# Gated projection of a graph network: products of pairs taken as seven of their own blocks' products, two at a time in shared PSUM banks that are refilled with sums

## The chip, the cores and the metric

One core of one Trainium2 chip. The metric is the device time of one execution in microseconds (us); the kernel before has a median of 2511.55 us over three runs (2511.07, 2511.55, 2512.0). Engines are called as the profile calls them: PE is TensorE's matmuls, PEld its weight loads, DVE VectorE, ACT ScalarE, POOL GpSimd, SP the queue that issues the DMAs.

## The reference

A pre-LN network on a graph of 1024 nodes with 512 features. A graph convolution, four layers, a graph convolution; the last output and two residuals are added. The layer, with LN for a layer norm with its weights:

```python
for i in range(4):
    h = h + _attn(LN2(h), cond, Wq[i], Wk[i], Wv[i], Wo[i])      # 16 groups of 64 nodes, 256 conditions each
    u = LN3(h) @ geglu_w[i] + geglu_b[i]                         # 1024 x 512 @ 512 x 4096
    val, gate = split(u, 2, axis=-1)
    f = val * gelu(gate)                                         # 1024 x 2048
    h = h + f @ ffo_w[i] + ffo_b[i]
```

The change concerns the second product, u, called the gated projection here. All of it is float32. The residual `base`, which the output stage adds at the very end, is relu(LN(x)) + x + gcn_out_b, and is made beside the layers.

## The kernel before

**Loops.** A layer l (of L = 4) first runs attention over eight groups of nodes g = 0 to 7, then the feed-forward part in R = 4 rounds r = 0 to 3. A round covers 512 of the 2048 columns of `val` and of `gate`, makes `f` for them (`geglu`), and adds its share of `f @ ffo_w` to h (`ffn_out`, two halves s = 0 and 1).

**Seven products.** Large matrix products are made by blocks of two by two, with seven block products in place of eight. The left factors are the weights `wval`, `wgate` and three sums of them (`ges`), made on GpSimd by `geglu_weights` for the next round; the right factors are the transposed normalised nodes `ln3T` and their sums `ln3S`. The products carry numbers 0 to 6 (the position in `order7`). One product for one block c of 128 columns is two matmuls of 128x512 (two contraction halves, `multiply`, L302), and it is collected in PSUM banks of 128x512 and combined by additions: value and gate of both halves of the nodes, f0 and f1, come out of seven products.

**Round 0** takes blocks c = 0 to 3 one after another (class `Quad`, `first`, `second`, `rest`).

**Rounds 1 to 3** take them in two pairs p = 0, 1 (class `Pair`), blocks p and p + 2 together: 24 pairs in the program. Here products 5 and 6 of the pair are made by seven products of their own blocks once more (`INNER = (5, 6)`): `Pair.seven` makes seven matmuls of 128x256 (L1021) which hold the answer for both blocks, with two banks e and f, each halved, and combines them by 128x256 operations (L1025 to L1038). The left factors of these inner products are further sums of the weights, made in `inner_lefts` on GpSimd for each round (three tiles, two inner products); the right ones are further sums of `ln3T` and `ln3S`, made in `inner_right_of` on GpSimd in round 0 and kept in `wos`, a tile that is free then. Products 0, 4, 3, 2 and 1 are direct: 20 matmuls of 128x512 for the two blocks. `Quad.end` finishes each block: the gate's sum (L964, L968), gelu on ScalarE (L933), the value's sum with its bias (L971), the product with the gate (L973, L975).

**After a block** `sums` in `geglu` makes the sums of f that `ffn_out` needs (L1083 to L1087); its last instruction, `geglu.last`, releases GpSimd for the next round's weights.

**ffn_out** is 14 products of four matmuls of 128x256, two halves of seven; its results are added to h (`hall`), s = 1 to blocks 2, 3, 6 and 7.

**The residual base** is made in the pairs of rounds 1 to 3, a block after each pair until eight are done: fetch x, Relu on ScalarE (L1396), two additions on GpSimd (L1398, L1399), a store to DRAM (L1400).

**Order.** Engines execute their own queues in order, and the order within them is the one in which the program issues, except where `issue_after` and `waiting_for` move something, and `keep_in_program_order` forbids it. `waiting_for(x, engine)` lets what follows on an engine stand after x. PSUM has eight banks, `bank(name)` gives the next; `acc_tile` gives one of six buffers of 128x512, `t512` one of ten; `slots_of` takes from 36 slots of 128x1024. `add_bias` adds the output bias row `ffb` to a block of h on GpSimd, for blocks 6 and 7 after round 0.

Of the kernel before, what the change touches and what calls it, by code (L numbers as in the profile page):

```python
# [8 lines left out]
F32 = mybir.dt.float32  # L9
# [5 lines left out]
OP = mybir.AluOpType  # L15
# [8 lines left out]
def gnn_kernel(  # L24
# [49 lines left out]
    rows = ctx.enter_context(tc.tile_pool(name="rows", bufs=2))  # L74
# [38 lines left out]
    def load_row(vec, offset, name):  # L113
        t = rows.tile([P, D], F32, tag="row", name=name)
# [182 lines left out]
    def multiply(to, left, right, cols_of, start):  # L297

        for n, (l0, l1, r0, r1) in enumerate(cols_of):
            at = to if len(cols_of) == 1 else to[:, n * (r1 - r0):(n + 1) * (r1 - r0)]  # L300
            for k in range(2):
                nc.tensor.matmul(at, left[:, k, l0:l1], right[:, k, r0:r1],  # L302
                                 start=start and n == 0 and k == 0,
                                 stop=n == len(cols_of) - 1 and k == 1, skip_group_check=True)
# [604 lines left out]
    class Quad:  # L909
# [49 lines left out]
        def end(self):  # L959

            n, c, bias = self.n, self.c, gcols[:, self.cv:self.cv + 1]
            pc, pd = bank(f"gc_{n}"), self.d
            g1 = t512(f"g1_{n}")
            nc.vector.tensor_tensor(g1, pd, self.u3, OP.add)  # L964
            self.gate(g1, n)
            self.product(3, pc, True)
            g0 = t512(f"g0_{n}")
            nc.vector.tensor_tensor(g0, pc, self.u3, OP.add)  # L968
            self.gate(g0, n)
            self.product(2, pd, False)  # L970
            nc.vector.scalar_tensor_tensor(self.u2, pd, bias, self.u2, OP.add, OP.add)  # L971
            f0, f1 = (self.fT[i][c // 2][:, c % 2, :] for i in range(2))
            nc.vector.tensor_tensor(f1, self.u2, g1, OP.mult)  # L973
            self.product(1, self.a, False)
            nc.vector.scalar_tensor_tensor(f0, self.a, bias, g0, OP.add, OP.mult)  # L975

# [13 lines left out]
    INNER = (5, 6)  # L990

    def inner_lefts(l, r, left):
        rooms = [t512(f"gi_{l}_{r}_{i}") for i in range(3)]
        rooms = [x[:, i * M:(i + 1) * M] for x in rooms for i in range(2)]
        return {i: inner_left(nc.gpsimd, left[i], *rooms[3 * n:3 * n + 3])
                for n, i in enumerate(INNER)}

    def inner_right_of(n, right):
        rooms = [wos[:, 2 * n + k, i * M:(i + 1) * M] for k in range(2) for i in range(2)]
        return inner_right(nc.gpsimd, right[INNER[n]], *rooms)  # L1000

    class Pair:

        def __init__(self, l, r, p, left, right, inner, fT):
            self.n, self.p, self.inner = f"{l}_{r}_{p}", p, inner
            self.quads = [Quad(l, r, c, left, right, fT) for c in (p, p + 2)]

        def seven(self, i):  # L1010

            n, p = f"{self.n}_{i}", self.p
            left, right = (x[i] for x in self.inner)
            e, f = bank(f"ge_{n}"), bank(f"gf_{n}")
            a, b, c, d = e[:, :M], e[:, M:], f[:, :M], f[:, M:]
            t = acc_tile(f"gt_{n}")
            to = self.w = [acc_tile(f"gw{q}_{n}") for q in range(2)]
            s1, u2 = t[:, :M], t[:, M:]

            def product(k, to, start):  # L1020
                nc.tensor.matmul(to, left[k][:, p * P:(p + 1) * P], right[k], start=start,  # L1021
                                 stop=True, skip_group_check=True)

            product(0, a, True)
            nc.scalar.copy(s1, a)  # L1025
            product(5, b, False)
            nc.vector.tensor_tensor(u2, b, s1, OP.add)
            product(6, c, True)
            nc.vector.tensor_tensor(s1, c, u2, OP.add)
# [11 lines left out]
        def run(self, sums, beside):  # L1041
            q0, q1 = self.quads
            for q in self.quads:
                q.a = bank(f"ga_{q.n}")
            q0.product(0, q0.a, True)
            steps = self.seven(5)
            next(steps)
            q1.product(0, q1.a, True)
            next(steps)
            for q, w in zip(self.quads, self.w):  # L1050
                q.u2 = w
                nc.vector.tensor_tensor(w, q.a, w, OP.add)
            steps = self.seven(6)
            next(steps)
            for q in self.quads:
                q.d = bank(f"gd_{q.n}")
            q0.product(4, q0.d, True)
            next(steps)
            for q, w in zip(self.quads, self.w):
                q.u3 = w  # L1060
                nc.vector.tensor_tensor(w, w, q.u2, OP.add)
            q1.product(4, q1.d, True)
            for q in self.quads:
                q.end()
                sums(q.c)
            beside(self.p)
# [10 lines left out]
    def geglu(quads, fT, s, begun, beside=lambda c: None):  # L1077
        def sums(c):
            k = c % 2
            a11, a12, a21, a22 = (fT[i][j][:, k, :] for i in range(2) for j in range(2))  # L1080
            s1, s2, s4 = (x[:, k, :] for x in s)
            if c < 2:
                nc.vector.tensor_tensor(a21, a11, a21, OP.subtract)  # L1083
            else:
                nc.vector.tensor_tensor(s2, a22, a21, OP.subtract)
                nc.vector.tensor_tensor(s1, s2, a11, OP.add)
                sums.last = nc.vector.tensor_tensor(s4, a12, s2, OP.subtract)  # L1087

        for c, q in enumerate(quads):
            if begun:  # L1090
                q.last = q.rest()()
                beside(c)
                sums(c)
            else:
                q.run(sums, beside)
        geglu.last = sums.last
        return order7([*fT[0], *fT[1]], *s)
# [164 lines left out]
    for l in range(L):  # L1262
# [63 lines left out]

        oTs = []
        for g in range(NG - 1):
# [8 lines left out]
            def between(last_key):  # L1337
# [9 lines left out]
                for nb in ready:  # L1347
                    add_bias(nb)

            if g or l:  # L1350
# [35 lines left out]
        fetched, rights = {}, {}  # L1386

        def fetch_x(nb):
            fetched[nb] = t512(f"x_again_{nb}")
            nc.sync.dma_start(fetched[nb], x[nb * P:(nb + 1) * P, :])  # L1390

        def base_of(nb):


            xt, xn = fetched.pop(nb), t512(f"again_{nb}")
            nc.scalar.activation(xn, xt, AF.Relu, bias=x_shift[:, nb:nb + 1],  # L1396
                                 scale=x_root[:, nb:nb + 1])
            nc.gpsimd.tensor_tensor(xt, xt, bias_out, OP.add)  # L1398
            nc.gpsimd.tensor_tensor(xt, xt, xn, OP.add)  # L1399
            nc.sync.dma_start(base_dram[nb], xt)  # L1400

        for r in range(R):
# [7 lines left out]
            if r:  # L1410
                fT, fS, quads = pairs_of(l, r, left, right, (lefts, rights))
                nb = 2 * (l * (R - 1) + r - 1)
                if nb < NB:
                    if nb == 0:
                        bias_out = load_row(gcn_out_b, 0, "bias_out")
                        nc.gpsimd.tensor_tensor(x_shift, x_mean.rearrange(
                            "p a (b c) -> p (a b) c", c=2)[:, :, 0], x_root, OP.mult)
                        nc.gpsimd.tensor_scalar(x_shift, x_shift, -1.0, None, OP.mult)
                    fetch_x(nb)
                    fetch_x(nb + 1)  # L1420
                    beside = lambda p: base_of(nb + p)
            else:
                wff = []

                def beside(c):
                    if c == 2:
                        wff.extend(out_weights(nc.vector, l, 0, raw_out))
                    elif c < 2:
                        with waiting_for(quads[c].last, mybir.EngineType.Pool):
                            rights[INNER[c]] = inner_right_of(c, right)  # L1430

            fT = geglu(quads, fT, fS, not r, beside)
            if r + 1 < R:
                raw_out = load_out(l, r + 1)
                with waiting_for(geglu.last, mybir.EngineType.Pool):
                    left = geglu_weights(l, r + 1, *raw)
                    lefts = inner_lefts(l, r + 1, left)
                    if not r:
                        for nb in range(NB - 2, NB):
                            add_bias(nb)  # L1440
                for s in range(2):
                    ffn_out(l, r, s, fT, wff, kept)
            else:
# [69 lines left out]
```

## Time and profile before

| | |
|---|---|
| median of three runs | 2511.55 us (2511.07 to 2512.0) |
| the profiled execution | 2511.2 us, of which the span that the profile shows is 2509.4 |
| PE busy | 2487.4 us, 99% |
| PEld | 1820.7 us, 73% |
| DVE | 1484.3 us, 59% |
| POOL | 619.8 us, 25% |
| ACT | 533.1 us, 21% |
| matmuls of the pairs, L302, by group `gd<-ln3S,ges` | 256 passes of 128x512, 128.1 us |
| matmuls of the inner seven, L1021, by group `ge<-ln3S,ges` | 96 passes of 128x256, 28.6 us |

A row of instructions gives line, engine, operation, output from inputs, the shape and the count, then busy time and the mean in ns of one, then the idle time of the engine ahead of it and what ended that. A row of a timeline begins with the start and the duration in us; one row may hold several instructions of a kind (x4). A float32 matmul shows as two instructions, called passes below. Matmul passes overlap in the pipeline, so a pass's own duration is longer than the distance to the next one's start.

### The profile page before, as it was taken

Reading aid. Unit: us, or ns where it says so; the run is one execution under the profiler, and the core shown is the slowest. Engines: PE = TensorE matmul, PEld = TensorE weight load, DVE = VectorE, ACT = ScalarE, POOL = GpSimd, SP = SyncE. Lnnn points to the kernel's source line nnn. Section 1 sums busy time; section 2 is a strip of 40 time slices with the busy share of each in tenths; the row PEclk is TensorE's granted clock in tenths of the full one; section 3 lists DMA queues with packets and bytes.
Section 4 is the critical chain, followed back from the end, with each engine's and each line's share of the span. In section 5 each row is a group of like instructions: output and inputs, shape, how many; then the busy total and the mean of one; then the engine's idle time right before and its main releaser. Section 6 shows DMA issues by size and latency. Waiting matters only on the chain. (4 is left out here: it accounts for less than half of the span.)

```text
span 2509.4 us, 33048 instructions
## 1 busy us (share of the span) xinstructions
PE 2487.4 (99%) x12752; PEld 1820.7 (73%) x12752; DVE 1484.3 (59%) x3265; ACT 533.1 (21%) x1318; POOL 619.8 (25%) x581
## 2 busy tenths in 40 slices
PE   8999999999999999999999999999999999999998
PEld 5778886666678887566687888566677888566665
DVE  9655565566664555666574555655574555665561
ACT  7322222111112222111112222211112222211111
POOL 1322223443220113332420113133401112233300
PEclk9999999999999999999999999999999999999999
DMA  6302232111211112020202222110121111111210
GB/s 180 132 30 93 93 110 68 47 68 34 105 59 61 59 64 68 23 86 17 97 30 76 72 64 59 43 43 26 51 76 59 60 62 65 43 42 51 84 34 34
DMA packets 69380, 161.06 MB, mean 64 GB/s; under 512 B 5768, under 2 KB 6096, under 8 KB 69216
## 3 DMA queue, kind: packets, MB, share of 16 engines
q1 hardware_dynamic: 67120, 153.44, 18.7%
q0 software_dynamic: 1376, 4.30, 0.5%
q8 instruction: 105, 1.72, 0.3%
q10 hardware_dynamic: 720, 1.11, 0.1%
q14 instruction: 59, 0.48, 0.1%
HBM read 135.76 MB, written 23.07 MB: 63 GB/s over the span
## 5 line engine op out<-in xcount | busy, mean ns | idle before, releaser
L302 PE MATMUL ga<-ln3T,wval 128*128 128x512 f32 x512 | 245.6, 593 | 0.0
L302 PEld LDWEIGHTS ga<-ln3T,wval 128*128 128x128 f32 x512 | 96.0, 190 | 89.5 <-issue 85.1
L933 ACT ACTIVATE g<-g,gcols 128x512 f32<-128x512 f32 x128 | 87.3, 716 | 328.8 <-DVE g L946 112.6
L777 ACT ACTIVATE pr<-sc,nmax 128x256 f32<-128x256 f32 x256 | 118.0, 473 | 176.7 <-DVE nmax L772 176.7
L302 PE MATMUL gd<-ln3S,ges 128*128 128x512 f32 x256 | 128.1, 592 | 0.0
L302 PE MATMUL pa_v<-wv,ct 128*128 128x256 f32 x512 | 123.1, 379 | 0.0
L220 POOL TENSOR_TENSOR ges<-wgate,wgate 128x1024 f32<-128x1024 f32 x16 | 37.7, 2353 | 344.3 <-DVE fs L1087 329.1
L302 PE MATMUL fa<-wff,fT 128*128 128x256 f32 x512 | 121.6, 379 | 0.0
L302 PE MATMUL pc_v<-wv,ct 128*128 128x256 f32 x512 | 121.0, 379 | 0.0
L302 PE MATMUL pc_k<-ct,wk 128*128 128x256 f32 x512 | 121.0, 379 | 0.0
L302 PE MATMUL pd_k<-ct,wks 128*128 128x256 f32 x512 | 121.0, 379 | 0.0
L302 PE MATMUL pd_v<-wvs,ct 128*128 128x256 f32 x512 | 120.9, 379 | 0.0
L302 PE MATMUL gd<-ln3T,ges 128*128 128x512 f32 x256 | 120.7, 594 | 0.1
L302 PE MATMUL gc<-ln3S,wgate 128*128 128x512 f32 x256 | 120.3, 592 | 0.0
L302 PE MATMUL pa_k<-ct,wk 128*128 128x256 f32 x480 | 116.2, 385 | 0.0
L302 PEld LDWEIGHTS fa<-wff,fT 128*128 128x128 f32 x512 | 97.3, 190 | 21.8 <-issue 9.1
L302 PEld LDWEIGHTS pc_k<-ct,wk 128*128 128x128 f32 x512 | 97.3, 190 | 13.2
L302 PEld LDWEIGHTS pd_v<-wvs,ct 128*128 128x128 f32 x512 | 97.3, 190 | 13.2
L302 PEld LDWEIGHTS pd_k<-ct,wks 128*128 128x128 f32 x512 | 97.3, 190 | 13.2
L302 PEld LDWEIGHTS pa_v<-wv,ct 128*128 128x128 f32 x512 | 97.1, 190 | 13.5 <-issue 0.4
L302 PEld LDWEIGHTS pc_v<-wv,ct 128*128 128x128 f32 x512 | 95.7, 190 | 12.2
L302 PEld LDWEIGHTS pa_k<-ct,wk 128*128 128x128 f32 x480 | 88.7, 190 | 21.3 <-issue 10.4
(354 smaller groups left out, 4962.3 us busy)
## 6 DMA issues: line engine op xcount, KB each, us to landing
ct<-cond_dram SPq DMA_DIRECT2D x72, 512.0 KB, 4.4
wval<-in_L_gnn_geglu_w_dram SPq DMA_DIRECT2D x32, 512.0 KB, 4.4
wgate<-in_L_gnn_geglu_w_dram SPq DMA_DIRECT2D x32, 512.0 KB, 4.7
wff<-in_L_gnn_ffo_w_dram SPq DMA_DIRECT2D x32, 512.0 KB, 4.0
cond_dram<-ct SPq DMA_DIRECT2D x24, 512.0 KB, 3.0
cond<-in_L_gnn_cond_dram SPq DMA_DIRECT2D x32, 256.0 KB, 4.5
ct<-cond_dram SPq DMA_DIRECT2D x24, 256.0 KB, 5.2
wk<-in_L_gnn_Wk_dram SPq DMA_DIRECT2D x8, 512.0 KB, 5.3
```

The lines of the kernel that those rows point to most:

```text
L220: t.tensor_tensor(s1, a21, a22, OP.add)
L302: nc.tensor.matmul(at, left[:, k, l0:l1], right[:, k, r0:r1], start=start and n == 0 and k == 0, stop=n == len(cols_of) - 1 and k == 1, sk ...
L777: nc.scalar.activation(pr3[:, a, :], ps3[:, a, :], AF.Exp, bias=nmax[:, a:a + 1], accum_out=tot[:, a:a + 1])
L933: nc.scalar.activation(pre, pre, AF.Gelu, bias=gcols[:, cg:cg + 1])
```

## The change

In rounds 1 to 3, products 0 and 4 of a pair are taken by inner sevens too: `INNER = (0, 5), (6, 4)`. `seven_of(two)` replaces `seven(i)`. It makes the seven inner products of two of the pair's products side by side, in four banks a to d, each holding 256 columns of the one and 256 of the other, and combines them by operations of 128x512. The results stand in `wos`, w for the first call and the same place for the second.

Products 1, 3 and 2 remain direct (12 matmuls of 128x512 for two blocks). They don't get banks of their own: after a `seven_of`, ScalarE copies sums back into its banks (L1057, L1059, L1065), and the direct products accumulate on top (`start=False`). So a bank ends with the finished value, and f is one operation per block and half (L1050) that reads it.

The matmuls of a pair are kept in program order. The sums of the first pair's f are issued within the second pair (after its second seven's last addition, L1067), those of the second at the round's end.

The tile `wos` being taken, the inner right factors live in four further slots (all 36 are then in use). Inner lefts take six tiles instead of three. The residual base moves from the pairs to attention, groups 1 and 2 of each layer; its additions are on VectorE, its buffers come from `acc_tile`. The shift `x_shift` is made on VectorE. The pool of bias rows has one buffer instead of two, with `bias_out` in one of its own. The output bias for blocks 6 and 7 is added in round 3, after its `geglu`, instead of round 0.

```diff
-    rows = ctx.enter_context(tc.tile_pool(name="rows", bufs=2))
+    rows = ctx.enter_context(tc.tile_pool(name="rows", bufs=1))
...
-    INNER = (5, 6)
+    INNER = (0, 5), (6, 4)
 
     def inner_lefts(l, r, left):
-        rooms = [t512(f"gi_{l}_{r}_{i}") for i in range(3)]
+        rooms = [t512(f"gi_{l}_{r}_{i}") for i in range(6)]
...
+        def seven_of(self, two):
+
+            p, (lefts, rights) = self.p, self.inner
+            a, b, c, d = (bank(f"g{x}_{self.n}_{two[0]}") for x in "abcd")
+            w = [wos[:, 2 * q:2 * q + 2, :] for q in range(2)]
+            s1, u2 = (acc_tile(f"g{x}_{self.n}_{two[0]}") for x in ("s", "u"))
 
             def product(k, to, start):
-                nc.tensor.matmul(to, left[k][:, p * P:(p + 1) * P], right[k], start=start,
-                                 stop=True, skip_group_check=True)
+                for n, i in enumerate(two):
+                    tc.keep_in_program_order(
+                        nc.tensor.matmul(to[:, n * M:(n + 1) * M],
+                                         lefts[i][k][:, p * P:(p + 1) * P], rights[i][k],
+                                         start=start and n == 0, stop=True, skip_group_check=True))
+
+            def add(to, x, y):
+                return nc.vector.tensor_tensor(to, of(x), of(y), OP.add)
...
             product(0, a, True)
             nc.scalar.copy(s1, a)
-            product(5, b, False)
-            nc.vector.tensor_tensor(u2, b, s1, OP.add)
+            product(5, b, True)
+            add(of(u2), b, s1)
             product(6, c, True)
-            nc.vector.tensor_tensor(s1, c, u2, OP.add)
-            product(4, d, False)
-            nc.vector.tensor_tensor(to[1][:, M:], d, s1, OP.add)
-            yield
+            add(of(s1), c, u2)
+            product(4, d, True)
+            add(w[1][:, :, M:], d, s1)
             product(1, a, False)
-            nc.scalar.copy(to[0][:, :M], a)
+            nc.scalar.copy(w[0][:, :, :M], of(a))
             product(3, c, False)
-            nc.vector.tensor_tensor(to[1][:, :M], c, u2, OP.add)
+            add(w[1][:, :, :M], c, u2)
             product(2, d, False)
-            nc.vector.tensor_tensor(to[0][:, M:], d, u2, OP.add)
-            yield
...
+            self.last = add(w[0][:, :, M:], d, u2)
+            return (a, b, c, d), [[x[:, n, :] for x in w] for n in range(2)]
...
+            def gated(q, of, w, name):
+                g = t512(f"{name}_{self.n}_{q}")
+                nc.vector.tensor_tensor(g, of, w, OP.add)
+                value, gate = biases(q)
+                nc.scalar.activation(g, g, AF.Gelu, bias=gate)
+
+                def times(to, x):
+                    nc.vector.scalar_tensor_tensor(to, x, value, g, OP.add, OP.mult)
+
+                return times
+
+            (a0, a1, c1, c0), (w1, w6) = self.seven_of(INNER[0])
+            a, c = (a0, a1), (c0, c1)
+            for q in (1, 0):
+                nc.scalar.copy(a[q], w1[q])
+                nc.vector.tensor_tensor(w6[q], a[q], w6[q], OP.add)
+                nc.scalar.copy(c[q], w6[q])
+            (*d, _, _), (w7, w5) = self.seven_of(INNER[1])
+            upper = {}
+            for q in (1, 0):
+                product(1, 1 - q, a[1 - q])
+                nc.vector.tensor_tensor(w5[q], c[q], w5[q], OP.add)
+                nc.scalar.copy(d[q], w5[q])
+                upper[q] = gated(q, d[q], w7[q], "g1")
+            with tc.issue_after(self.last.ins):
+                sums()
+            f = [[self.fT[i][n // 2][:, n % 2, :] for n in self.cols] for i in range(2)]
+            for q in range(2):
+                product(3, q, c[q])
+                gated(q, c[q], w7[q], "g0")(f[0][q], a[q])
+            for q in range(2):
+                product(2, q, d[q])
+                upper[q](f[1][q], d[q])
...
+        def base_of(nb):
+
+
+            xt, xn = fetched.pop(nb), acc_tile(f"again_{nb}")
+            nc.scalar.activation(xn, xt, AF.Relu, bias=x_shift[:, nb:nb + 1],
+                                 scale=x_root[:, nb:nb + 1])
+            nc.vector.tensor_tensor(xt, xt, bias_out, OP.add)
+            nc.vector.tensor_tensor(xt, xt, xn, OP.add)
+            nc.sync.dma_start(base_dram[nb], xt)
...
+                if g in (1, 2):
+                    base_of(2 * l + g - 1)
+
+            if g in (1, 2):
+                fetch_x(2 * l + g - 1)
...
+                with waiting_for(geglu.last, mybir.EngineType.Pool):
+                    for nb in range(NB - 2, NB):
+                        add_bias(nb)
                 ffn_out(l, r, 0, fT, wff, kept)
```

More of the change, by code (lines that the diff above doesn't have):

```diff
@@ L957, in rest @@
             return lambda: nc.vector.scalar_tensor_tensor(f0, self.a, bias, g0, OP.add, OP.mult)
[L959 to L975, printed above, removed]
     def inner_left(t, x, s1, s2, s4):
@@ L1007, in __init__ @@
             self.n, self.p, self.inner = f"{l}_{r}_{p}", p, inner
[L1008 to L1018, printed above, removed]
-            def product(k, to, start):
-                nc.tensor.matmul(to, left[k][:, p * P:(p + 1) * P], right[k], start=start,
-                                 stop=True, skip_group_check=True)
+            self.cols = [p, p + 2]
@@ L1094, in geglu @@
             else:
-                q.run(sums, beside)
+                q.run(sums_of_made)
+                made.extend(q.cols)
+        sums_of_made()
         geglu.last = sums.last
@@ L1385, in gnn_kernel @@
         kept = slot(f"kept_{l}")
[L1386 to L1400, printed above, removed]
+        rights = {}
         for r in range(R):
```

93 lines of the change are left out of this document (41 added, 52 removed).

## The prediction

> **What bounds the kernel now.** I read the page first, then TensorE's waits, then windows in three stages, and last the timeline of one pair of round 1.
>
> ```profile
> span 2509.4 us, 33048 instructions
> PE 2487.4 (99%) x12752; PEld 1820.7 (73%) x12752; DVE 1484.3 (59%) x3265; ACT 533.1 (21%) x1318; POOL 619.8 (25%) x581
> PEclk9999999999999999999999999999999999999999
> ```
>
> TensorE is busy for 2487.4 of 2509.4 us; no other engine passes 60%. Is the rest spread over the span or at its ends?
>
> ```profile
> PE edges L394 <- DVE high L380: 3.8, 1, 3.8
> ...
> PE deg L498 <- DVE sums L497: 0.5, 1, 0.5
> ```
>
> The view of TensorE's waits has ten rows, all of lines 302 to 656, each met once or twice: the graph stages at start and end. None is of the layers' projections.
>
> ```profile
> 488.00:560.00 72.00, 72.00 (x255) 47.98 (x254) 44.02 (x72) 9.72 (x18) 29.31 (x24) 1.00 0.19 66
> 800.00:900.00 100.00, 100.00 (x724) 86.52 (x723) 53.51 (x128) 24.51 (x73) 12.71 (x17) 1.00 0.19 64
> 1100.00:1200.00 100.00, 100.00 (x354) 66.80 (x353) 62.48 (x102) 12.22 (x22) 32.84 (x24) 1.00 0.11 37
> ```
>
> Columns: length, then busy time of PE, PEld, DVE, ACT, POOL, the clock granted, DMA. In a gated round (first row), in attention (second) and in a later stretch (third) TensorE is busy for the whole window at clock 1.00. So between the ends a matmul saved is its whole time saved, and each moment that TensorE waits is its whole time lost. Removing work from VectorE, ScalarE or GpSimd is worth nothing by itself.
>
> **What a matmul costs.** The timeline of one pair gives spacings; the durations in it overlap, so I use starts.
>
> ```profile
> 501.90 1.88 PE L302 MATMUL gc<-ln3S,wgate 128*128 128x512 f32 x4
> ...
> 506.20 1.02 PE L302 MATMUL ga<-ln3T,wval 128*128 128x512 f32 x2
> ...
> 513.92 0.59 PE L1021 MATMUL ge<-ln3S,ges 128*128 128x256 f32 x2
> ...
> 535.41 1.89 PE L302 MATMUL fa<-wff,fT 128*128 128x256 f32 x8
> ...
> 559.59 1.45 PE L302 MATMUL ga<-ln3T,wval 128*128 128x512 f32 x3
> ```
>
> A float32 matmul shows as two passes. Between 501.90 and 513.92 lie 28 passes of 512 columns (a pair's last seven products over two halves): 12.02/28 = 0.4293 us. Between 535.41 and 559.59, an output stage, lie 14 products of 8 passes of 256: 24.18/112 = 0.2159, and 1.727 for a product. So a matmul takes 0.8586 us at 512 columns and 0.4318 at 256, slightly more than half.
>
> **The change on TensorE.** There are 4 layers x 3 rounds x 2 = 24 pairs. In each, products 0 and 4 of two column blocks over two halves, 8 matmuls of 512 columns, become 2 x 7 = 14 of 256 (in the built program 192 fewer and 336 more). Removed 8 x 0.8586 = 6.869 us, added 14 x 0.4318 = 6.045: 0.824 less, of 20 x 0.8586 + 14 x 0.4318 = 23.22. Times 24: **19.8 us** less. With a short pass 1 ns shorter or longer it would be 0.7 us more or less.
>
> **Does TensorE stay without gaps?** Now banks are reused within a pair, so hand-offs to ScalarE and VectorE stand close to TensorE. Their rows:
>
> ```profile
> 493.07 0.42 DVE L1027 TENSOR_TENSOR gt<-ge,gt 128x256 f32<-128x256 f32 x1 [3.18 <-PE ge L1021]
> 493.53 0.42 DVE L1029 TENSOR_TENSOR gt<-gf,gt 128x256 f32<-128x256 f32 x1
> ...
> 503.36 0.69 DVE L964 TENSOR_TENSOR g<-gd,gw 128x512 f32<-128x512 f32 x1
> 503.97 0.68 DVE L968 TENSOR_TENSOR g<-gc,gw 128x512 f32<-128x512 f32 x1
> ...
> 506.40 0.75 DVE L971 SCALAR_TENSOR_TENSOR gw<-gd,gcols,gw 128x512 f32<-128x512 f32 x1 [1.15 <-PE gd L302]
> 507.24 1.45 DVE L973 TENSOR_TENSOR fT<-gw,g 128x512 f32<-128x512 f32 x1
> ...
> 511.73 0.69 DVE L973 TENSOR_TENSOR fT<-gw,g 128x512 f32<-128x512 f32 x1
> ```
> ```profile
> 504.14 1.95 ACT L933 ACTIVATE g<-g,gcols 128x512 f32<-128x512 f32 x3 [4.25 <-DVE g L964]
> ```
> ```profile
> 493.55 0.37 PEld L1021 LDWEIGHTS ge<-ln3S,ges 128*128 128x128 f32 x2 [0.49 <-DVE gt L1027]
> ```
> ```profile
> L1025 ACT COPY gt<-ge 128x256 f32<-128x256 f32 x48 | 17.9, 372 | 321.8 <-PE ge L1021 321.8
> L731 ACT COPY v<-pa_v 128x512 f32<-128x512 f32 x31 | 18.1, 585 | 193.6 <-PE pa_v L302 193.6
> L933 ACT ACTIVATE g<-g,gcols 128x512 f32<-128x512 f32 x128 | 87.3, 716 | 328.8 <-DVE g L946 112.6 <-DVE g L964 102.2 <-DVE g L968 97.2
> L1083 DVE TENSOR_TENSOR fT<-fT,fT 128x512 f32<-128x512 f32 x32 | 25.3, 789 | 0.8
> L220 POOL TENSOR_TENSOR ges<-wgate,wgate 128x1024 f32<-128x1024 f32 x16 | 37.7, 2353 | 344.3 <-DVE fs L1087 329.1 <-DVE pr L782 9.4 <-DMA cond_dram<-ct 5.9
> L222 POOL TENSOR_TENSOR gi<-gi,wgate 128x256 f32<-128x256 f32 x12 | 8.7, 727 | 0.0
> L213 POOL TENSOR_TENSOR wffs<-wff 128x512 f32<-128x512 f32 x12 | 15.2, 1271 | 0.0
> ```
>
> Hops: TensorE's slot end to VectorE 506.20 to 506.40, 0.20 us, and I take ScalarE alike. VectorE's end to ScalarE 504.05 to 504.14, 0.09, taken for the way back too. VectorE to a VectorE operation that needs it 493.49 to 493.53, 0.04; independent ones start 0.60 apart. VectorE's end to the weight load 493.49 to 493.55 and the load, 0.25. An addition of 128x512 takes 0.69, a copy out of PSUM 0.585. **The refill, a ScalarE copy into PSUM, is in no row.** Its nearest rows are the copy of half the size from below (0.372) and the gelu from above (0.716); far off, a GpSimd operation of that size, 1.271. I take 0.585, the same engine, size and operation with the ends exchanged, and keep 0.372 and 1.27 as ends; by the lower one nothing changes, since slack grows.
>
> Now a pair with 0 at its first matmul. The first seven for two products ends at 6.05, the second at 12.09; direct products 1 end at 15.52, 3 at 18.96, 2 at 22.39. Three places are tight.
>
> *Second seven, bank c.* The first seven's last addition (L1012) runs 6.25 to 6.94; ScalarE refills a (L1057) 7.03 to 7.61, and only behind that copies the next seven's first bank (L1018), 7.61 to 8.20; additions that need one another run 8.29 to 8.98 and 9.02 to 9.71; with 0.25 TensorE may accumulate into c at 9.96, and comes there, five slots of 0.864 after 6.05, at 10.36. Slack 0.40.
>
> *Direct product 3 into c.* That seven's addition out of c (L1012) runs 11.43 to 12.12, the addition L1064 on it 12.16 to 12.85, the seven's last 12.76 to 13.45, the refill of d (L1065) meanwhile 12.94 to 13.52, the gate's sum (L1045) 13.61 to 14.30, the other L1064, which reads the bank that product 3 wants, 14.21 to 14.90, with 0.25 at 15.15. TensorE comes at 15.52: slack 0.37. In a second pair the built order puts the first pair's subtraction L1092 ahead of that gate's sum: started at 13.36, it holds VectorE for 0.71 (its mean is 0.10 over the others'), so the sum starts at 14.07, the other L1064 ends at 15.36, and 15.61 is **0.08 late**: 12 x 0.08 = 1.0 us.
>
> *Round's end.* Two operations on f and four sums stand behind the last matmul. The second output product (24.11) needs L1092, done at 22.99 + 0.25: slack 0.87. The third, at 25.84, needs L1095, done at 25.11 + 0.25: slack 0.48.
>
> **The rest of the change.** Per round GpSimd makes 16 instead of 8 inner sums of 128x256 of the weights (in round 0 also 16 for 8 of the inputs, 16 x 0.727 = 11.6 us, read only after the output stage). It starts them when the round's last sum is done, about 3.4 us after the output stage begins, where it was
>
> ```profile
> 538.36 2.35 POOL L220 TENSOR_TENSOR ges<-wgate,wgate 128x1024 f32<-128x1024 f32 x1 [5.33 <-DVE fs L1087]
> ```
>
> 538.36 - 535.41 = 2.95 before. Up to the first sum that TensorE needs it has 4 x 2.35 + 7 x 0.727 + 1.27 = 15.8, so 19.2; the output stage lasts 24.18 and product 5 comes 0.86 later. Slack 5.8. The last sums, 27, meet a need at 24.18 + 6.05 + 0.86 = 31.1. If GpSimd's operations took a quarter longer, the first would still be in time. The additions of the bias to blocks 6 and 7, moved to round 3 and waiting on GpSimd for the round's last sum, are 2 x 1.27 from 3.4, done near 6; the output stage's second half, which adds to those blocks, starts at 12. Behind them in GpSimd's queue stand sums for the next layer's weights, which are wanted after the whole output stage. The next layer's bias row waits for its one buffer, and is wanted a layer later. Nothing of it costs.
>
> The residual base (16 additions of 128x512) leaves GpSimd for VectorE in attention:
>
> ```profile
> L302 PE MATMUL pc_v<-wv,ct 128*128 128x256 f32 x512 | 121.0, 379 | 0.0
> ```
>
> Those 512 passes are 16 for each of 32 projections: a product lasts 16 x 0.2159 = 3.45 us. Two additions are 2 x 0.79 = 1.6 us in front of one that frees a bank for a following product, on an engine with 53.51 of 100 us busy. Taken as hidden; uncovered it is 16 x 0.79 = 12.6 us. On SP's queue the base's store waits for these additions ahead of the loads of the block after next; seven products, 24 us, of the next block lie between, and the additions would have to be that late to matter.
>
> The addition L973, both of whose inputs lie in SBUF, took 0.69 us at 511.73 but 1.45 at 507.24, beside this:
>
> ```profile
> 506.87 1.26 POOL L1398 TENSOR_TENSOR x_again<-x_again,bias_out 128x512 f32<-128x512 f32 x1 [15.00 <-ACT again L1396]
> ```
>
> The moved additions have two such inputs too: at 1.45 the uncovered price is 23.2 us, and two of them, 2.9 us, still fit a product's 3.45. The Trainium skill, "SBUF — State Buffer", section "Who interferes with whom", has this as a rule: a VectorE instruction with two SBUF inputs contends with a GpSimd instruction that reads SBUF, one with a single such input does not. By that rule, the trace agrees.
>
> **The sum.** 2511.2 (the profiled execution: its span of 2509.4 and 1.8 around it) - 19.8 + 1.0 = 2492.4; that execution stood 0.35 under the median 2511.55, so **2492.8**.
>
> **Rivals.** *B, VectorE becomes the bound at the bank hand-offs.* For it: slacks of 0.4 are two hops wide, the bank's turn-round is a chain of five operations that no row of before shows end to end, L973's 1.45 is what a subtraction such as L1092 costs beside GpSimd, and VectorE has 26 operations of some 0.7 us in a second pair, 18 of 22.4 us (44.02 of 72 in the window of before). Against it: GpSimd's sums end at 27, long before a second pair begins at 24.18 + 22.39 = 46.6. If L1092 takes 1.45, the second pairs are late by 0.08 + 0.76: 12 x 0.84 = 10.1, 2501.9. If each chain is 0.5 us longer, first pairs lose 0.10 + 0.13, second 0.10 + 0.58: 12 x 0.91 = 10.9, **2502.7**.
>
> *C, slower: the refill copies.* A write into PSUM that takes x longer than 0.585 counts twice in the chain to the second seven, since two refills of a stand ahead of the copy there (the first ends at 6.75, the next starts at 7.03: 2x - 0.28 - 0.40), and once before product 3 (x - 0.37). The pair loses its 0.824 at 3x = 1.87: a refill of 0.585 + 0.625 = **1.21 us** is the point from which it is slower. At 1.27, x = 0.685: 0.69 + 0.31 = 1.00 per pair, 24.1 us, **2515.8**; at twice the gelu's 0.716, 2527. Against it: no ScalarE row of this size exceeds 0.72.
>
> The Trainium skill, "ScalarE: Activation LUTs", section "Step-by-step: what each stage is for", holds that PSUM is the lower-latency destination for ScalarE. No row here shows it; by it the refill is under 0.585, C falls away, and the sum stays, since in second pairs L1092 holds VectorE.
>
> *D, no gain in the passes.* It then doesn't do what it says. Short passes leave 0.2159 - 0.189 = 27 ns for the weight load, and in the pairs some loads stand idle for a releaser (11.7 us in the row of L1021's loads). If each of the 56 short passes took 0.824/56 = 15 ns more, the gain would be gone: **2511.5**. Against it: the pairs of before have such loads and no TensorE idle time, and 112 short passes in a row kept 0.2159.
>
> **How the numbers follow.** Forecast 0.69, B 0.20, C 0.07, D 0.04. The measurement tells 0.2%, 5 us, from no change: under 2506.5 is faster, which holds the forecast and nearly all of B (0.89); no change is D with a mild C (0.04); slower is C (0.07). The forecast's own range is 2490 to 2495: down without the lateness (1.0), by 0.7 for the spacings and 0.5 for the spread of the runs before, which makes 2490.6, rounded down; up by twice the lateness and the same two. Upwards the range reaches to B, 2503. C and D, 0.11, are left out.
>
> **What would show it.** Right would be: TensorE's waits without a row of the pairs, or one at L302 met about 12 times for 0.1 us; a pair's first matmul 22.4 us after the last one's; refills (L1057, L1059, L1065) near 0.585; L1092 at 0.69 in second pairs. Refills over 0.9, or TensorE waits on L1012, L1064 or L1018 in all pairs, would show it wrong; so would windows in attention, or at the start of a round's pairs, with TensorE below 100%.

## The result and the profile after

| | before | after |
|---|---|---|
| median of the runs | 2511.31 us (2509.79 to 2512.0, four runs) | 2491.39 us (2490.8 to 2492.21, four runs) |
| the profiled execution | 2511.2 us, span 2509.4 | 2491.68 us, span 2489.9 |

The changed kernel takes 0.9922 of the time (95% interval 0.9905 to 0.9939): 19.9 us less. The forecast was 2492.8 in 2490.0 to 2503.0, and 2492.4 for a profiled execution.

The page of the kernel after, its first two lines:

```profile
span 2489.9 us, 33837 instructions
...
PE 2468.3 (99%) x13040; PEld 1877.5 (75%) x13040; DVE 1517.5 (61%) x3235; ACT 635.5 (26%) x1462; POOL 686.4 (28%) x691
```

Of the span's 19.5 us, TensorE's busy time gave 19.1, with 288 more passes. ScalarE and GpSimd do 102 and 67 us more and VectorE 33, and TensorE waits for none of it in the layers. The waits of TensorE (line, who ended it, total, times, longest), first and last row of eleven:

```profile
PE edges L395 <- DVE high L381: 3.8, 1, 3.8
...
PE tr_x L184 <- DVE x L172: 0.2, 1, 0.2
```

There is still no row of the layers' projections. The same three windows as before (length; PE, PEld, DVE, ACT, POOL; clock; DMA):

```profile
488.00:560.00 72.00, 72.00 (x288) 54.37 (x287) 45.22 (x68) 17.49 (x29) 29.83 (x31) 1.00 0.15 46
800.00:900.00 100.00, 100.00 (x723) 86.47 (x722) 55.47 (x138) 25.81 (x75) 14.74 (x18) 1.00 0.22 77
1100.00:1200.00 100.00, 100.00 (x395) 74.73 (x394) 63.78 (x97) 20.90 (x34) 43.40 (x41) 1.00 0.12 34
```

TensorE is at 100% in all three, so the time must have gone out of the number and length of its passes. One round in the timeline of TensorE, kernel after, from the first pair's start through the second pair and the output stage to the next pair:

```profile
489.24 0.59 PE L1007 MATMUL ga<-ln3T,wval 128*128 128x256 f32 x2
...
501.32 1.88 PE L302 MATMUL ga<-ln3T,wval 128*128 128x512 f32 x4
...
511.62 0.59 PE L1007 MATMUL ga<-ln3T,wval 128*128 128x256 f32 x2
...
527.14 1.88 PE L302 MATMUL gd<-ln3S,wgate 128*128 128x512 f32 x4
...
534.01 1.89 PE L302 MATMUL fa<-wff,fT 128*128 128x256 f32 x8
...
558.18 0.59 PE L1007 MATMUL ga<-ln3T,wval 128*128 128x256 f32 x2
```

The first pair takes 511.62 - 489.24 = 22.38 us (22.39 before rounding), the second 22.39; its two sevens end 12.09 us after its start, and direct product 3 starts at 527.14, 15.52 into the pair. The forecast had 22.39, 12.09 and 15.52, with 15.61 for product 3 in second pairs. The same round before began here:

```profile
489.00 1.88 PE L302 MATMUL ga<-ln3T,wval 128*128 128x512 f32 x4
```

and ended at 559.59, the output stage's end that the prediction quotes: 70.59 us, against 68.94 now. That is 1.65 us in two pairs, and 12 rounds make 19.8. The whole gain is there. Between the last matmuls of one output stage and the next, all twelve such rounds of the profile after take 68.95 us, and eleven of the twelve before 70.59 (one takes 71.00). All first pairs of the profile after last 22.39 us, and second pair and output stage together 46.56 in each of the eight rounds that another round of pairs follows.

How the hand-offs stand to TensorE, VectorE's timeline in that second pair (511.62 is its start):

```profile
524.38 0.68 DVE L1012 TENSOR_TENSOR wos<-gd,gu 128x512 f32<-128x512 f32 x1
524.98 0.68 DVE L1092 TENSOR_TENSOR fT<-fT,fT 128x512 f32<-128x512 f32 x1
525.57 0.68 DVE L1045 TENSOR_TENSOR g<-gb,wos 128x512 f32<-128x512 f32 x1
526.17 0.68 DVE L1064 TENSOR_TENSOR wos<-gd,wos 128x512 f32<-128x512 f32 x1
```

L1092 starts at 13.36, as forecast. But it holds the queue for 0.59 us, not 0.71, so L1064 ends at 15.23 instead of 15.36. In a first pair, where L1092 doesn't stand, the rows of VectorE and ScalarE show the hops around the refill of d:

```profile
501.38 0.69 DVE L1064 TENSOR_TENSOR wos<-gc,wos 128x512 f32<-128x512 f32 x1
...
502.11 0.59 ACT L1065 COPY gb<-wos 128x512 f32<-128x512 f32 x1 [1.68 <-DVE wos L1064]
...
502.73 0.69 DVE L1045 TENSOR_TENSOR g<-gb,wos 128x512 f32<-128x512 f32 x1
```

From VectorE's end to ScalarE's start it is 0.04 us, and back 0.03; the forecast had 0.09 for each. The groups of instructions (busy us and the mean ns of one stand between the bars) give the price that no row of before showed:

```profile
L1026 ACT COPY wos<-ga 128x512 f32<-128x512 f32 x48 | 28.1, 585 | 105.1 <-PE ga L1007 105.1
...
L1059 ACT COPY gc<-wos 128x512 f32<-128x512 f32 x24 | 14.2, 593 | 0.0
L1065 ACT COPY gb<-wos 128x512 f32<-128x512 f32 x24 | 14.2, 591 | 40.2 <-DVE wos L1064 40.2
L1057 ACT COPY gb<-wos 128x512 f32<-128x512 f32 x24 | 14.2, 590 | 23.2 <-DVE wos L1012 23.2
```

A refill takes 590 to 593 ns, a copy out of PSUM 585. The forecast had taken 585.

### The profile page after: what moved, and what is told of

Read it like the earlier page. It is cut to its first block, busy times and chain, and to the rows that moved or that the text cites. A ratio compares the mean times of both kernels' runs of the same rounds, so it can differ in the third digit from the quotient of the medians.

```text
span 2489.9 us, 33837 instructions
## 1 busy us (share of the span) xinstructions
PE 2468.3 (99%) x13040; PEld 1877.5 (75%) x13040; DVE 1517.5 (61%) x3235; ACT 635.5 (26%) x1462; POOL 686.4 (28%) x691
## 5 line engine op out<-in xcount | busy, mean ns | idle before, releaser
L1342 POOL TENSOR_TENSOR hall<-hall,ffb 128x512 f32<-128x512 f32 x32 | 41.0, 1287 | 322.3 <-DVE xn_ln L172 238.3
L302 PE MATMUL ga<-ln3T,wval 128*128 128x512 f32 x224 | 104.4, 594 | 0.0
L1018 ACT COPY gs<-ga 128x512 f32<-128x512 f32 x48 | 27.9, 582 | 287.6 <-PE ga L1007 287.6
L849 POOL TENSOR_TENSOR os<-oT 128x256 f32<-128x256 f32 x12 | 8.7, 728 | 317.3 <-DVE oT L824 317.3
L1047 ACT ACTIVATE g<-g,gcols 128x512 f32<-128x512 f32 x96 | 69.3, 722 | 94.8 <-DVE g L1045 94.8
L773 DVE TENSOR_REDUCE nmax<-sc 128x2 f32<-128x512 f32 x128 | 83.0, 680 | 10.2 <-PE sc L766 10.2
```

Source lines behind the costliest of these rows:

```text
L302: each(nc.tensor.matmul(at, left[:, k, l0:l1], right[:, k, r0:r1], start=start and n == 0 and k == 0, stop=n == len(cols_of) - 1 and k == ...
L773: nc.vector.tensor_reduce(nmax, ps3, AX.X, OP.max, negate=True)
L849: t.tensor_tensor(s1, a21, a22, OP.add)
L1047: nc.scalar.activation(g, g, AF.Gelu, bias=gate)
L1342: nc.gpsimd.tensor_tensor(h[nb], h[nb], ffb, OP.add)
```

## The experiments

All run beside the kernel before on the same chip, whose median was 2510.93, 2511.93 or 2511.28 us in the three sets. "Over the changed kernel" means over its 2491.39 from the set of the result. The kernel before moved by up to 1.0 us between sets, so a difference of one or two us rests on the lengths of pairs and rounds in the trace, not on the medians.

### The parts around the pairs, alone

```diff
 kernel before
-                    beside = lambda p: base_of(nb + p)
...
+                if g in (1, 2):
+                    base_of(2 * l + g - 1)
```

> The kernel before with one part of the change alone: the residual base made in attention on VectorE, one row buffer, the output bias of blocks 6 and 7 added in round 3. The pairs are as before. If the forecast's step is right that all of this is hidden, the time is that of before, 2511.3 us within 1, and TensorE's waits have no row of the attention. If the two additions are uncovered, 16 x 0.79 = 12.6 us more. If the change gained by this part and not by its matmuls, the time falls towards 2491.

Measured: 2510.97 us, ratio 1.0001 (0.9992 to 1.0010). The residual base in attention, the single row buffer and the late bias cost nothing and bring nothing that could be measured (the interval reaches some 2.3 us to each side). So the gain is that of the pairs, and the price of 12.6 us for uncovered additions falls.

### What a short pass costs

```diff
-                         [(self.cols[q] * P, (self.cols[q] + 1) * P, 0, 512)], False,
+                         [(self.cols[q] * P, (self.cols[q] + 1) * P, m * M, (m + 1) * M)
+                          for m in range(2)], False,
```

> The changed kernel with each direct matmul of 128x512 in the pairs as two of 128x256: 12 become 24 per pair, the columns are the same. By the spacings (0.8586 and 0.4318) a pair takes 12 x 0.005 = 0.06 us more, 24 pairs 1.4 us: 2492.8. If short passes in a pair cost 15 ns more each than the forecast takes (rival D), 48 passes x 24 pairs x 0.015 = 17 us more. If a short pass costs exactly half, no change.

Measured: 2493.05 us (2492.09 to 2493.39), 1.7 over the changed kernel, against 1.4 expected and 17 by rival D. In its profile the direct part of a pair takes 10.36 us instead of 10.30: 0.06, the third digit of the spacings. Here columns are paid for and hardly instructions: 288 more matmuls cost 1.7 us. That is why taking products as sevens of half-width matmuls gains nearly the full eighth (0.824 of 6.869 us).

### The subtraction ahead of the hand-off

```diff
-            with tc.issue_after(self.last.ins):
+            with tc.issue_after(read.ins):
                 sums()
```

where `read` is the second L1064.

> The changed kernel, with the first pair's subtraction L1092 moved behind the second L1064 of the second pair. The forecast put it 0.08 us in the way in each of 12 second pairs, 1.0 us; the profile after shows no TensorE wait there and L1092 at 0.59 in the queue, so now: 2491.4, no change within 0.7 us, and the first L1064 to product 3 gets 0.6 us of slack. If hand-offs of VectorE bind as rival B has it, the time falls by several us.

Measured: 2491.47 us (2490.98 to 2492.04). No change: the hand-off wasn't late.

```diff
             if c < 2:
-                nc.vector.tensor_tensor(a21, a11, a21, OP.subtract)
+                if not begun:
+                    tc.keep_in_program_order(
+                        nc.vector.tensor_tensor(s1, a11, a21, OP.subtract))
+                tc.keep_in_program_order(nc.vector.tensor_tensor(a21, a11, a21, OP.subtract))
```

The gate's sums and the last addition of a seven are kept in program order too, and `sums()` is issued right behind the second seven. The added line runs for both pairs of a round, so the sums at the round's end come later as well.

> The changed kernel with one more VectorE subtraction of 128x512 ahead of the second L1064 in the second pairs (its result is not used), and the first pair's other sums kept behind it. By the profile after, L1064 there ends 15.23 us into the pair, its load and matmul follow at 15.52, and TensorE comes at 15.52: no slack at all. So 0.60 more in the queue costs 12 x 0.6 = 7.2 us: 2498.6, with a TensorE wait on L1064 met 12 times for 0.6. If there were slack of 0.4 as in first pairs, 12 x 0.2 = 2.4; if the hand-off doesn't set TensorE at all, nothing.

Measured: 2494.25 us (2493.04 to 2494.69), 2.9 over the changed kernel instead of 7.2, and no wait on L1064. That expectation was wrong, and TensorE's timeline of this kernel shows why:

```profile
527.67 0.59 PE L302 MATMUL fa<-wff,fT 128*128 128x256 f32 x2
528.11 0.59 PE L302 MATMUL fc<-wff,fT 128*128 128x256 f32 x2
528.54 1.88 PE L302 MATMUL gd<-ln3S,wgate 128*128 128x512 f32 x4
```

Two matmuls of the output stage, one of fa and one of fc whose inputs the first pair had finished, stand ahead of product 3 (`gd`). Only the pairs' matmuls are kept in program order; the output stage's may be placed earlier than the program issues them, and here they put 0.87 us of work where a wait of about 0.5 would have been. What the edit did cost is 0.19 us in each of 12 rounds (46.75 for 46.56), all of it in the output stage. So the run doesn't measure the slack. A later pair of runs does (below).

### Later by a known time: the copy of the second seven

```diff
-            nc.scalar.copy(s1, a)
+            for _ in range(2 if two == INNER[1] else 1):
+                nc.scalar.copy(s1, a)
```

> The changed kernel with the copy of the second seven's first bank (L1018) made a second time, behind the two refills of c on ScalarE: its end moves from 8.12 to about 9.64 us into the pair, 1.52 later. With the forecast's slack of 0.40 on bank c, TensorE waits 1.1 us in each of 24 pairs: 26 us, 2517, on L1012 or its queue. If there is no slack 36 us; if the hand-off is not what TensorE would wait for next, nothing.

Measured: 2514.21 us (2513.83 to 2514.75), 22.8 over the changed kernel. Its waits and TensorE's timeline:

```profile
PE gc L1007 <- DVE gs L1012: 9.4, 24, 0.4
```
```profile
498.68 0.70 PE L1007 MATMUL ga<-ln3T,wgate 128*128 128x256 f32 x2
499.21 0.59 PE L1007 MATMUL ga<-ln3S,ges 128*128 128x256 f32 x2
500.20 0.70 PE L1007 MATMUL gc<-gr,wgate 128*128 128x256 f32 x2 [0.39 <-DVE gs L1012]
```

and ScalarE's and VectorE's in the same pair:

```profile
496.52 0.58 ACT L1019 COPY gs<-ga 128x512 f32<-128x512 f32 x1
...
498.04 0.58 ACT L1019 COPY gs<-ga 128x512 f32<-128x512 f32 x1
```
```profile
499.45 0.69 DVE L1012 TENSOR_TENSOR gs<-gc,gu 128x512 f32<-128x512 f32 x1
```

The second copy starts 1.52 us after the first. The wait is at the place that the forecast named, bank c, in all 24 pairs. The row at 498.68 is late too, since the second copy reads its bank a, but what a pair loses is set by the later place. A first pair lasts 23.36 us and a second one with its output stage 47.53, 0.97 more each for a delay of 1.52, so the copy had a slack of 0.55.

The addition out of c has less. In the changed kernel it ends 9.72 us into the pair (498.96), here 11.17 (500.14): 1.45 later, not 1.52, since there the chain's first addition also had to wait for VectorE, which was free only after the copy's end (497.49 against 497.36). So bank c had a slack of 1.45 - 0.97 = 0.48, where the forecast had 0.40. The rows say where the difference lies: VectorE ends at 500.14, the matmul stands at 500.20, 0.06 later, and its first pass takes 0.10 longer (the row has 0.70, the one before it in these rows 0.59). From VectorE's end to a pass on schedule that makes 0.16, where the forecast had 0.25. The chain's end was forecast at 9.71.

### Less work ahead of the tight place, and behind it

```diff
-                         tc.keep_in_program_order)
+                         tc.keep_in_program_order, 1 if i == 1 else 2)
```

with the last argument the number of contraction halves; the second run has 2 for 1.

> The changed kernel with the second contraction half of direct product 1 left out: 2 of 4 matmuls per pair, 2 x 0.8586 x 24 = 41.2 us of TensorE's work, taken away ahead of product 3. If TensorE's work alone sets the time, 2450. By the forecast's chain to product 3, which can't start before 15.07 us into a first pair and 15.52 into a second one, only 0.44 x 12 = 5 us are gained: 2486, and TensorE waits on L1064 in all pairs for 1.3 and 1.7 us.

> The changed kernel with the second contraction half of direct product 2 left out: the same 41.2 us of TensorE's work, but behind the tight place. The next pair's banks are free early, so first pairs gain all of it. At a round's end f's sums then come late for the second and third output product: L1092 by 0.66, L1095 by 0.38 more, 1.04 x 12 = 12.5 us. So 2491.4 - 41.2 + 12.5 = 2463. If the sums aren't in the way, 2450; if the chain through the banks binds everywhere, about 2486 as with product 1.

Measured: 2474.92 us (16.5 less than the changed kernel) and 2450.68 (40.7 less), for the same work left out. Without half of product 1, waits and timeline of TensorE:

```profile
PE gd L302 <- DVE wos L1064: 15.8, 24, 0.9
```
```profile
503.33 1.02 PE L302 MATMUL gb<-ln3T,wval 128*128 128x512 f32 x2
505.23 1.98 PE L302 MATMUL gd<-ln3S,wgate 128*128 128x512 f32 x4 [0.88 <-DVE wos L1064]
...
526.00 0.59 PE L302 MATMUL fa<-wff,fT 128*128 128x256 f32 x2
526.43 0.62 PE L302 MATMUL fc<-wff,fT 128*128 128x256 f32 x2
527.49 1.98 PE L302 MATMUL gd<-ln3S,wgate 128*128 128x512 f32 x4 [0.44 <-DVE wos L1064]
```

Of 1.72 us taken away, a first pair gains 0.57 (it lasts 21.81 us): that is its slack. The chain to product 3 is the next bound, and it is near. A second pair with its output stage gains 0.88 (45.68 for 46.56). Its product 3 stands 15.29 us into the pair and loses 0.10 on its first pass: 0.13 earlier than 15.52, which is the slack of a second pair. The rest is output work, since two matmuls of 0.43 again stand in the wait. The place is right, the sizes were not: 16.5 between the medians (17.4 by the rounds) for an expected 5.

Without half of product 2 everything is gained. The 1.04 us per round of late sums didn't come, by the same filling, in that run's timeline:

```profile
532.58 0.59 PE L302 MATMUL fc<-wff,fT 128*128 128x256 f32 x2
533.02 0.59 PE L302 MATMUL fd<-wffs,fs 128*128 128x256 f32 x2
533.45 1.46 PE L302 MATMUL fc<-wff,fT 128*128 128x256 f32 x6
```

One matmul of fc, then one of fd from the next product, and only then the rest of fc, which reads the late sum.

### The same with the output stage in order

```diff
-                     [((2 * s + q) * P, (2 * s + q + 1) * P, 0, M) for q in range(2)], start)
+                     [((2 * s + q) * P, (2 * s + q + 1) * P, 0, M) for q in range(2)], start,
+                     tc.keep_in_program_order)
```

in the changed kernel, in the one with the second subtraction, and in the one without half of product 2.

> The changed kernel with the output stage's matmuls kept in program order, as a base for the next two. In the profile after, TensorE has no wait in the pairs or the output stage of rounds 1 to 3, and only two short passes of an output product stand early (in round 0). If that order isn't what hides the hand-offs there: no change, 2491.4 within 1. If the output stage's reordering had been hiding the late sums of f, 12 to 16 rounds x 0.4 = 5 to 6 us more.

> The kernel with the extra subtraction in the second pairs (e4), with the output matmuls kept in order. In e4 four short passes of the output stage stood ahead of product 3 and filled the wait. Without them L1064 ends at 15.83 us into the second pair, with 0.16 (the 0.06 to the load and the 0.10 that the first pass takes longer, as in the run with half of product 1) at 15.99, and TensorE comes at 15.52: 0.47 in 12 pairs, 5.6 us, 2497; up to 0.5 more at the round's end, where the extra subtraction delays the sums too (2503). If e4 was that fast because the hand-off has slack, it stays at 2494.

> The kernel with half of product 2 left out (e9), with the output matmuls kept in order. The sums of f then must be late: L1092 ends 2.40 us into the output stage, its matmul is due at 1.73 + 0.43 = 2.16, so 0.40 late with 0.16; L1095 some 0.2 more: 12 x 0.6 = 7 us, 2458. If the sums are early enough by themselves, 2450.7 as before.

Measured: 2492.71 us (2492.26 to 2494.28), 2504.35 (2503.39 to 2505.29) and 2459.38. The first is 1.3 over the changed kernel. Its pairs of rounds 1 to 3 are the changed kernel's, 22.39 and 46.56. The difference stands in round 0, where a wait on L944 appears four times, once per layer: from a layer's last pair to the next layer's first it takes 0.43 longer, 1.7 in four layers. So in the changed kernel as it is, nothing in the pairs is hidden by reordering. The second, TensorE's timeline:

```profile
527.37 1.98 PE L302 MATMUL gd<-ln3S,wgate 128*128 128x512 f32 x4 [0.21 <-DVE wos L1066]
...
536.07 2.17 PE L302 MATMUL fc<-wff,fT 128*128 128x256 f32 x8
538.07 2.09 PE L302 MATMUL fd<-wffs,fs 128*128 128x256 f32 x8
540.00 1.89 PE L302 MATMUL fb<-wffs,fs 128*128 128x256 f32 x8
```

Product 3 was due at 527.00, 1.72 after product 1's second half at 525.28, and comes at 527.37 with 0.10 on its first pass: 0.47 late, as expected. The output products fc and fd take 2.00 and 1.93 us instead of 1.73: 0.47 more for the late sums. Together 0.95 in each of 12 rounds (46.56 becomes 47.51), 11.4 us (11.6 between the medians). From 0.60 more in the queue came 0.47, so a second pair has 0.13 of slack, as the run without half of product 1 says too. The third is 8.7 over its counterpart; the trace gives 1.7 of round 0 again, and 0.61 in each of 12 rounds (45.45 for 44.84), where 0.6 was expected.

### GpSimd's room

```diff
+        for _ in range(4 if r else 0):
+            nc.gpsimd.tensor_tensor(s[0], wgate[0], wgate[1], OP.add)
         sums_of_a(nc.gpsimd, *wval, *wgate, *s)
```

> The changed kernel with four more GpSimd sums of 128x1024 (results rewritten by the same value) ahead of the next round's inner sums in rounds 1 to 3: 4 x 2.35 = 9.4 us. The first inner sum that TensorE needs is done 6.3 us ahead of need in the profile after (5.8 by the forecast), so TensorE waits 3.1 us in 12 rounds: 37 us, 2528. If GpSimd were already the bound, 12 x 9.4 = 113 us; if its sums had much more room, nothing.

Measured: 2542.07 us (2539.38 and 2544.76), 50.7 over the changed kernel, not 37. Waits, and TensorE's timeline in rounds 1 and 2:

```profile
PE gb L1009 <- POOL gi L222: 37.2, 12, 4.2
```
```profile
494.29 1.22 PE L1009 MATMUL gb<-gr,gi 128*128 128x256 f32 x2 [4.16 <-POOL gi L222]
495.30 1.06 PE L1009 MATMUL gc<-gr,wval 128*128 128x256 f32 x2
496.16 1.06 PE L1009 MATMUL gc<-gr,ges 128*128 128x256 f32 x2
...
568.91 0.70 PE L1009 MATMUL gb<-gr,gi 128*128 128x256 f32 x2 [2.58 <-POOL gi L222]
569.45 0.59 PE L1009 MATMUL gc<-gr,wval 128*128 128x256 f32 x2
```

The waits are the 37 that were expected, in 12 rounds: 4 x 4.16 + 8 x 2.58. In GpSimd's timeline of the kernel after, the first inner sum that TensorE needs is this one, in rounds 1 and 2:

```profile
484.46 0.73 POOL L222 TENSOR_TENSOR gi<-gi,ges 128x256 f32<-128x256 f32 x1
...
551.83 0.72 POOL L222 TENSOR_TENSOR gi<-gi,ges 128x256 f32<-128x256 f32 x1
```

It ends at 485.19 and 552.55, and the matmul that reads it, the pair's fourth, stands 1.30 us into the pair, at 490.54 and 559.48. With 0.16 for the hand-off that leaves 5.2 and 6.8 us; the forecast had 5.8. Most of what the waits leave of the 50.7 is the clock, by the windows of this run in round 1 of the first layer (length, busy times, the clock behind POOL's):

```profile
490.00:494.00 4.00, 0.13 (x1) 0.00 (x0) 0.00 (x0) 0.32 (x1) 4.00 (x6) 0.90 0.84 259
494.00:496.00 2.00, 1.71 (x4) 1.44 (x5) 0.38 (x1) 0.00 (x0) 2.00 (x4) 0.50 0.00 0
...
500.00:505.00 5.00, 5.00 (x25) 4.41 (x24) 3.30 (x6) 3.22 (x6) 4.12 (x4) 0.99 0.00 0
```

Before the wait of 4.16 us ends the granted clock has fallen (0.90 over 490 to 494); from 494 until about 500 it is 0.50, and matmuls start 0.86 apart instead of 0.43. This first pair lasts 29.64 us, 7.25 over 22.39, and those of round 1 in the other three layers about 28.5, 6.1 over, of which 4.16 are the wait. The first pairs of rounds 2 and 3, with a wait of 2.58 and a clock that stays at 1.00, last 25.23, 2.84 over. So 0.26 more than the wait is lost without any change of the clock: 0.10 on the first pass, and 0.16 because the profile counts the wait from the modelled end of the matmul before. That makes 7.25 + 3 x 6.1 + 8 x 2.84 = 48.3 us; the profiled execution is 47.7 longer (span 2537.6 for 2489.9). The other run of this kernel has no profile. It is 5.4 us longer, at a mean granted clock of 0.994 against 0.997.

## Why the prediction was right, point by point

**What bounds the kernel.** Right: no wait of TensorE in the pairs before or after, the windows at 100%, and leaving out half of product 2 gave 40.7 of its 41.2 us.

**The passes.** The forecast took 19.8 us from 0.8586 and 0.4318 us per matmul. The rounds give 1.65 for two pairs, 12 x 1.65 = 19.8, and splitting matmuls cost 0.06 per pair as these numbers say. Rival D falls.

**Bank c in the second seven.** Right place, 24 of 24 waits when it was made late. Slack 0.48 instead of 0.40: the chain's end came out as forecast (9.72 for 9.71), the step from VectorE to TensorE is shorter.

**Direct product 3.** Here a term was mis-sized: the forecast had second pairs 0.08 us late, 1.0 us in all, and they aren't. In second pairs two numbers made it. L1092 was taken at 0.71 in the queue from the mean of before, which holds those that ran beside GpSimd's additions (0.98 us long at 509.38 of the profile before, beside L1399, and 0.69 in later rounds with none); in second pairs GpSimd is idle, and it is 0.59. And the step from VectorE to TensorE is 0.16, not 0.25. Together 0.21: slack 0.13 (measured by the ordered run and by the one without half of product 1) for -0.08. In first pairs L1092 doesn't stand in the way; there the two hops around the refill of d, 0.04 and 0.03 instead of 0.09 each, and the 0.09 of the last step make the slack 0.57 (by the run without half of product 1) for 0.37. Each of these numbers was taken too long, so the forecast's slacks erred on the safe side. This is most of the 1.4 us between 2492.8 and 2491.39; the rest is within the spread of the runs.

**The refill.** Taken at 0.585, measured 0.590 to 0.593, far from the 1.21 from which rival C has the change slower. The 0.585 was a choice between rows of before, none of which showed a refill, and it held. The Trainium skill, "ScalarE: Activation LUTs", section "Step-by-step: what each stage is for", has PSUM as ScalarE's lower-latency destination. The rows here show no gain by it: a copy of 128x512 into PSUM took 590 to 593 ns, out of PSUM into SBUF 585. They differ in the source too, so they don't single out the destination. The measurement decides, and for the time it made no difference.

**Rival B** falls as to the changed kernel, but it wasn't far: a VectorE queue that is 0.6 longer, with TensorE in order, costs 0.95 per round, and L1092 at 1.45 would cost (0.86 - 0.13) x 12 = 8.8 us at the hand-off alone, worked out and not run.

**Round's end.** No wait, as forecast. The reason that was given was too simple, though: the first matmul of an output product reads the first pair's half of the sums, which is ready long before. The late sum is needed only by the second matmul, 0.43 us later, so the real slack is larger by that (the 0.6 for the ordered run without half of product 2 was worked out that way). Besides, the output stage's matmuls can be reordered.

**The rest.** The moved base costs nothing (1.0001). GpSimd's room was given as 5.8 us and is 5.2 in round 1 and 6.8 in rounds 2 and 3.

## What to carry to other kernels

Where one engine is busy without gaps, count its passes to the third digit and check every new hand-off against the moment at which that engine comes by; here both came out of one timeline of the kernel before, and a pair's length came out to 0.01 us. Read the price of an operation from the instances that run under the same neighbours, not from the group's mean: 0.71 against 0.59 changed the sign of a slack. And before testing a slack by a delay, look at what else the engine may do in the gap: an order that is free to change fills it, and the delay then measures that.

## What the runs showed of the hardware that wasn't expected

A wait of TensorE can cost more than its length. With 4.16 us without work the granted clock fell to 0.50. In the first layer it stayed there for some six us, and the pair lost 2.8 us beside the wait and the 0.26 that every such wait costs; in the other three layers 1.7. With 2.58 us it stayed at 1.00. The Trainium skill, "TensorE: Matmul & The Clock Gate", section "What's actually happening", gives an idle window of about 3.4 us after which the clock is halved. The trace agrees with it on both sides: 4.16 lies above, 2.58 below. Nothing of this enters the changed kernel, whose waits in the layers are none.
